# Block rows of a mixture of experts: loaded whole and turned by TensorE, or loaded in four shares and turned by VectorE

## The chip, the cores and the metric

The kernel runs on one core of one Trainium2 chip. The metric is the device time of one execution in microseconds, the lower the better. A core has five engines with an instruction queue each: PE (TensorE, matrix products; its weight loads are listed as PEld), DVE (VectorE), ACT (ScalarE), POOL (GpSimd) and SP (SyncE, which here issues DMAs). Each works its own queue in order and waits on semaphores that the others raise.

## The reference, cut to what matters

Everything is fp32. A layer on 8 x 512 tokens of width 256 runs through four residual parts: a linear scan, a mixture of experts, a causal attention with 16 heads, and the same mixture of experts again.

```python
x = x + _L0_attn_a_ref(_layernorm(x), ...)     # scan
x = x + _L0_ffn_ref(_layernorm(x), ...)        # mixture of experts, first time
x = x + _L0_attn_b_ref(_layernorm(x), ...)     # attention
x = x + _L0_ffn_ref(_layernorm(x), ...)        # mixture of experts, second time
```

A mixture of experts chooses 4 of 16 experts for every token, with a factor for each choice:

```python
h = jnp.einsum('td,edf->etf', x, gate_w)
u = jnp.einsum('td,edf->etf', x, up_w)
y = jnp.einsum('etf,efd->etd', jax.nn.silu(h) * u, down_w)
routed = jnp.einsum('etd,te->td', y, combine)      # combine: the factors, zero where not chosen
sh = jax.nn.silu(x @ sh_gate_w) * (x @ sh_up_w) @ sh_down_w
return routed + sh
```

Widths: 256 in, 256 inside an expert, 256 out.

## The kernel before, in words

Two stretches alternate with two routed stages. A stretch (the scan, later the attention) also norms the tokens, computes the shared expert and the choices, and sends each normed token row by an indirect DMA of POOL into the DRAM tensor `xg`, once for each of its four experts, so that the rows of one expert lie together. A row has `ROW` = 272 columns: 256 of the token, 4 factors, 4 expert numbers, 8 copies of the token's number.

A routed stage, `routed(i, ...)`, then goes through `xg` in blocks of `BLK` = 128 rows, each block of one expert. It runs 136 blocks (`LIKELY`; 7 more stand under a condition on the number of blocks that are needed). Where a block's rows lie and which expert's weights it takes is read from two small tables into registers (`values`, L830). For a block n:

- `load(n)` (L850): SP copies the 128 rows of 1,088 bytes from `xg` into a buffer `rows` with one row per partition. The buffers are those of the tag `kb4`, nine of them (`KB`), so block n takes that of block n - 9, whose scatter has to have landed.
- `fetch(n)` (L863): ScalarE copies the gate weights of the block's expert, VectorE the up weights, from the place in `w_all` that a register names into a fixed buffer (tag `col`, six buffers, so three blocks).
- `turn(n)` (L878): the products need the token's columns on the partitions. TensorE transposes the two halves of 128 columns into PSUM, `pt`, and ScalarE copies them into columns `ROW` and on of the same buffer.
- `up(n)` (L885): eight products 128x128x128 into `ph`, gate half and up half; ScalarE takes the sigmoid of the gate half (L901), VectorE multiplies twice (L902, L903), which makes `act`; VectorE forms the row factor, `gain`, from the row's factors and expert numbers (L906, L914).
- `down(n)` (L917): two products of `act` with the down weights into `pyr`, four passes on TensorE; ScalarE scales by `gain` (L929); POOL adds the rows to the DRAM tensor `part` by an indirect DMA (L930).

`run` (L940) writes these in the order load(n + 2), fetch(n + 1), up(n), turn(n + 1), down(n - 2), and some other work at given blocks (`beside`: norms for the next stretch, sums of finished tokens). That is the order of the program's text; the compiler's scheduler settles each engine's own order from it, except where `tc.issue_after` or `tc.keep_in_program_order` pins an instruction.

The 16 experts' weights are loaded whole into `w_all` by SP long before a routed stage (`load_expert`, L216): for the gate and up weights the input row 128 k + p goes to partition p, so each piece is one row of 1,024 bytes.

Of the kernel before, what the change touches and what calls it, by code (L numbers as in the profile page):

```python
# [31 lines left out]
EG, TKG, TK = 4, 2, 4  # L32
# [3 lines left out]
BLK = P  # L36


NBLK = (TK * NTOK - E) // BLK + E
# [3 lines left out]
LIKELY = TK * NTOK // BLK + E // 2  # L43
NROW = E * REG + BLK
ROW = D + 2 * TK + 8
# [13 lines left out]
PACE = 2  # L59
SENT = 4  # L60
HELD = 6


SUMMED = {0: DONE[0], 1: 76, 2: 88, 3: 110, 4: 127}
# [12 lines left out]
def tile_hybrid_block(  # L77
# [22 lines left out]
    nc = tc.nc  # L100
# [23 lines left out]
    xg = [dram.tile([NROW, ROW], FP, name=f"xg_{i}") for i in range(2)]  # L124
# [41 lines left out]
    ident = const.tile([P, P], FP, name="ident")  # L166
# [49 lines left out]
    def load_expert(e: int):  # L216
        at = e * WEXP
        gu = w_all[:, at : at + 2 * KD * F].rearrange("p (s k f) -> p s k f", k=KD, s=2)
        nc.sync.dma_start(out=gu[:, 0], in_=gate_w[e].rearrange("(k p) f -> p k f", p=P))
        nc.sync.dma_start(out=gu[:, 1], in_=up_w[e].rearrange("(k p) f -> p k f", p=P))  # L220
        nc.sync.dma_start(
            out=w_all[:, at + 2 * KD * F : at + WEXP].rearrange("p (k d) -> p k d", k=KF),
            in_=down_w[e].rearrange("(k p) d -> p k d", p=P),
        )
# [5 lines left out]
        out=before,  # L230
        in_=before,
# [20 lines left out]
    def load_attention_weights():  # L252
# [16 lines left out]
        out=causal, in_=causal, compare_op=ALU.is_ge, fill=0.0, base=0, pattern=[[0, 2], [1, P]], channel_multiplier=-1  # L269
# [6 lines left out]
        out=tri, in_=tri, compare_op=ALU.is_gt, fill=0.0, base=0, pattern=[[1, P]], channel_multiplier=-1  # L276
# [546 lines left out]
    def routed(i: int, table, beside):  # L823

        weight_at, row_at, expert, many, _ = table
        ACT, DVE = mybir.EngineType.Activation, mybir.EngineType.DVE
        PE, SP = mybir.EngineType.PE, mybir.EngineType.SP
        held = {}

        def values(n: int):  # L830

            many = min(4, (LIKELY if n < LIKELY else NBLK) - n)
            _, w = nc.values_load_multi_w_load_instructions(
                weight_at[:, n : n + many],
                engines=[PE, ACT, DVE],
                min_val=0,
                max_val=(E - 1) * WEXP,
                skip_runtime_bounds_check_because="a count of at most E - 1 experts, times WEXP",
            )
            _, r = nc.values_load_multi_w_load_instructions(  # L840
                row_at[:, n : n + many],
                engines=[SP],
                min_val=0,
                max_val=NROW - BLK,
                skip_runtime_bounds_check_because="the blocks table stays within the sorted rows",
            )
            for j in range(many):
                held[n + j] = [w[j], r[j]]

        def load(n: int):  # L850
            if n not in held:
                values(n)
# [7 lines left out]
            nc.sync.dma_start(out=rows[:, 0:ROW], in_=xg[i][bass.ds(held[n][1], BLK), :])  # L860
            held[n].append(rows)

        def fetch(n: int):  # L863


            if n == 0:

                both = xpool.tile([P, NT, D], FP, tag="x", name=f"both_{i}").rearrange("p t d -> p (t d)")
            for half, (copy, name) in enumerate(((nc.scalar.copy, "gate"), (nc.vector.tensor_copy, "up"))):
                if n == 0:  # L870
                    here = both[:, half * KD * F : (half + 1) * KD * F]
                    copy = nc.vector.tensor_copy
                else:
                    here = work.tile([P, KD * F], FP, tag="col", name=f"{name}_{i}_{n}", bufs=COLS)
                copy(here, w_all[:, bass.ds(held[n][0] + half * KD * F, KD * F)])  # L875
                held[n].append(here)

        def turn(n: int):  # L878
            rows = held[n][2]
            pt = bank([P, KD, P], f"pt_{i}_{n}", "misc")  # L880
            for k in range(KD):
                nc.tensor.transpose(pt[:, k, :], rows[:, k * P : (k + 1) * P], ident)  # L882
            nc.scalar.copy(rows[:, ROW : ROW + D], pt.rearrange("p k q -> p (k q)"))  # L883

        def up(n: int):  # L885
            _, _, rows, *both = held[n]


            ph = bank([P, 2, KF * P], f"ph_{i}_{n}", "big")
            for s in range(2):  # L890
                for f in range(KF):
                    for k in range(KD):
                        nc.tensor.matmul(  # L893
                            ph[:, s, f * P : (f + 1) * P],
                            lhsT=both[s][:, k * F + f * P : k * F + (f + 1) * P],
                            rhs=rows[:, ROW + k * P : ROW + (k + 1) * P],
                            start=(k == 0),
                            stop=(k == KD - 1),
                        )
            act = rows[:, ROW + D : ROW + D + F]  # L900
            nc.scalar.activation(act, ph[:, 0, :], AF.Sigmoid)  # L901
            nc.vector.tensor_mul(act, ph[:, 0, :], act)  # L902
            nc.vector.tensor_mul(act, ph[:, 1, :], act)  # L903

            gain = small.tile([P, TK + 1], FP, tag="gain", name=f"gain_{i}_{n}", bufs=4)
            nc.vector.scalar_tensor_tensor(  # L906
                gain[:, 0:TK],
                rows[:, D + TK : D + 2 * TK],
                expert[:, n : n + 1],
                rows[:, D : D + TK],  # L910
                ALU.is_equal,
                ALU.mult,
            )
            nc.vector.tensor_reduce(gain[:, TK : TK + 1], gain[:, 0:TK], AX.X, ALU.add)  # L914
            held[n][3:] = [act, gain]

        def down(n: int):  # L917
            w, _, rows, act, gain = held.pop(n)
            py = bank([P, D], f"pyr_{i}_{n}", "y")
            for f in range(KF):  # L920
                nc.tensor.matmul(  # L921
                    py,
                    lhsT=act[:, f * P : (f + 1) * P],
                    rhs=w_all[:, bass.ds(w + 2 * KD * F + f * D, D)],
                    start=(f == 0),
                    stop=(f == KF - 1),
                )

            nc.scalar.mul(rows[:, 0:D], py, gain[:, TK : TK + 1])  # L929
            nc.gpsimd.indirect_dma_start(  # L930
                out=parts[i][n % 2],
                out_offset=bass.IndirectOffsetOnAxis(
                    ap=rows[:, D + 2 * TK : D + 2 * TK + 1].bitcast(U32), axis=0
                ),
                in_=rows[:, 0:D],
                in_offset=None,
                compute_op=ALU.add,
            )

        def run(first: int, last: int):  # L940
            load(first)
            load(first + 1)
            fetch(first)
            turn(first)
            for n in range(first, last + 2):
                if n + 2 < last:
                    load(n + 2)
                if n + 1 < last:
                    fetch(n + 1)
                if n < last:  # L950
                    up(n)
                if n + 1 < last:
                    turn(n + 1)
# [12 lines left out]

    def shared_experts(i: int, b: int, xnT_of, tanh: bool):
# [454 lines left out]
    with banks_of(big=4, misc=2, y=2):  # L1422
# [68 lines left out]
        def at_the_end(b: int):  # L1491
# [4 lines left out]
            engines=[mybir.EngineType.SP, mybir.EngineType.Activation, mybir.EngineType.DVE],  # L1496
# [52 lines left out]
```

## Time and profile before

| | us |
|---|---|
| three runs | 1734.45, 1742.05, 1742.82 |
| median | 1742.05 |
| the profiled execution | 1735.83 |
| its span, first to last instruction | 1734.1 |

| part of the span | us from the start |
|---|---|
| scan stretch | 0 to 351 |
| routed stage 0, up products of 136 blocks | 351 to 741 |
| attention stretch | 741 to 1306 |
| routed stage 1 | 1306 to 1701 |
| last sums and stores | 1701 to 1734 |

The profile is one execution recorded by the hardware. A row of it names the line of the kernel, the engine, the operation, the tiles written and read, and the mean time of one instruction; the idle time in front of it is given with the engine or DMA that ended it. One fp32 matrix product appears as two passes. A busy share is a mean over stages with different limits, so the routed stages are read by themselves.

### The profile page before, as it was taken

How to read it: one execution, taken by the hardware profiler on the slowest of the kernel's cores; microseconds unless marked ns; L12 is line 12 of the kernel's file. 1: busy time of each engine (PE TensorE's matmuls, PEld its weight loads, DVE VectorE, ACT ScalarE, POOL GpSimd, SP SyncE). 2: the span in 40 equal slices, each digit the busy share in tenths (PEclk: the TensorE clock that was granted, in tenths of full speed). 3: DMA queues.
4: the chain of work that ended last, by engine and by line, in shares of the span. 5: the costliest groups of instructions: out<-in, count | busy, mean ns of one | idle time of the engine just before them, and what ended most of it. 6: DMA issues, size and time to landing. Idle time of an engine off the chain costs nothing. (4 is left out here: it accounts for less than half of the span.)

```text
span 1734.1 us, 32869 instructions
## 1 busy us (share of the span) xinstructions
PE 1648.4 (95%) x10640; PEld 1225.8 (71%) x10640; DVE 1110.7 (64%) x3463; ACT 788.7 (45%) x1724; POOL 773.0 (45%) x675
## 2 busy tenths in 40 slices
PE   6899998999999999999999999999998999998993
PEld 3566655589999999944445545544558999998992
DVE  7888877545556655566776676676754755565562
ACT  3223232155555555555544454364315555554551
POOL 3356556435555555530042332332543555555563
PEclk8999999999999999999999999999999999999997
DMA  4454423445555665531011212122544555566666
GB/s 160 147 179 151 148 93 121 153 95 95 96 95 104 105 101 95 106 62 38 25 65 50 77 51 72 55 73 84 192 138 89 96 96 97 111 138 124 122 120 166
DMA packets 149277, 181.37 MB, mean 105 GB/s; under 512 B 16144, under 2 KB 135984, under 8 KB 149104
## 3 DMA queue, kind: packets, MB, share of 16 engines
q0 software_dynamic: 54720, 82.57, 25.6%
q1 hardware_dynamic: 92576, 92.71, 17.9%
q10 hardware_dynamic: 1808, 3.93, 0.6%
q8 instruction: 89, 1.46, 0.4%
q14 instruction: 84, 0.69, 0.1%
HBM read 81.62 MB, written 97.53 MB: 103 GB/s over the span
## 5 line engine op out<-in xcount | busy, mean ns | idle before, releaser
L930 POOL DMA_INDIRECT part<-rows x272 | 425.9, 1566 | 341.5 <-ACT rows L929 236.7
L723 POOL DMA_INDIRECT xg<-sorted_m,slots_m x256 | 258.3, 1009 | 267.6 <-ACT slots_m L720 91.9
L893 PEld LDWEIGHTS ph<-rows,gate 128*128 128x128 f32 x2160 | 282.0, 191 | 16.1 <-ACT rows L883 1.9
L893 PE MATMUL ph<-rows,gate 128*128 128x128 f32 x2160 | 285.5, 275 | 0.6 <-ACT rows L883 0.6
L893 PE MATMUL ph<-rows,up 128*128 128x128 f32 x2160 | 285.3, 275 | 0.0
L921 PE MATMUL pyr<-w_all,rows 128*128 x1088 | 279.8, 380 | 0.4 <-DVE rstd_l L431 0.4
L893 PEld LDWEIGHTS ph<-rows,up 128*128 128x128 f32 x2160 | 262.9, 192 | 0.0
L901 ACT ACTIVATE rows<-ph 128x256 f32<-128x256 f32 x272 | 104.2, 383 | 328.5 <-PE ph L893 328.5
L902 DVE TENSOR_TENSOR rows<-ph,rows 128x256 f32<-128x256 f32 x272 | 115.2, 424 | 190.4 <-ACT rows L901 189.4
L921 PEld LDWEIGHTS pyr<-w_all,rows 128*128 128x128 f32 x1088 | 185.5, 190 | 14.9 <-ACT rows L929 0.8
L875 ACT COPY gate<-w_all 128x512 f32 x270 | 168.8, 626 | 14.2 <-PE ph L893 2.4
L1131 ACT ACTIVATE w_all<-ps_a 128x1024 f32<-128x1024 f32 x128 | 124.4, 1021 | 68.8 <-PE ps_a L1120 63.7
L875 DVE COPY up<-w_all 128x512 f32 x270 | 118.1, 437 | 30.3 <-PE ph L893 17.5
L929 ACT ACTIVATE rows<-pyr,gain 128x256 f32<-128x256 f32 x272 | 128.4, 472 | 14.3 <-PE pyr L921 12.2
L906 DVE SCALAR_TENSOR_TENSOR gain<-rows,expert_b 128x4 f32<-128x4 f32 x272 | 61.2, 225 | 107.9 <-ACT rows L929 82.4
L1120 PE MATMUL ps_a<-w_all 32*128 32x384 f32 (+3 forms) x1024 | 120.0, 468 | 8.0 <-ACT w_all L1131 6.3
L982 PE MATMUL pg_m<-xT_m,su_sb 128*128 128x512 f32 x256 | 123.4, 604 | 0.0
L982 PE MATMUL pg_m<-xT_m,sg_sb 128*128 128x512 f32 x256 | 122.3, 599 | 0.0
L903 DVE TENSOR_TENSOR rows<-ph,rows 128x256 f32<-128x256 f32 x272 | 115.0, 423 | 8.4
L1011 PE MATMUL pd_m<-sd_sb,act_m 128*128 128x256 f32 x512 | 120.0, 382 | 0.0
L1011 PEld LDWEIGHTS pd_m<-sd_sb,act_m 128*128 128x128 f32 x512 | 95.4, 190 | 22.0 <-issue 5.7
L882 PE MATMUL pt<-ident,rows 128*128 128x128 f32 x544 | 103.7, 273 | 6.2 <-DMA rows<-xg 4.8
(228 smaller groups left out, 2176.7 us busy)
## 6 DMA issues: line engine op xcount, KB each, us to landing
rows<-xg SPq DMA_DIRECT2D x272, 136.0 KB, 2.5
part<-x SPq DMA_DIRECT2D x16, 512.0 KB, 2.9
part<-ys_m SPq DMA_DIRECT2D x14, 512.0 KB, 3.1
w_all<-in_L_ffn_gate_w_dram SPq DMA_DIRECT2D x24, 256.0 KB, 5.4
w_all<-in_L_ffn_up_w_dram SPq DMA_DIRECT2D x24, 256.0 KB, 5.4
w_all<-in_L_ffn_down_w_dram SPq DMA_DIRECT2D x24, 256.0 KB, 5.8
sum<-part POOLq DMA_DIRECT2D x10, 512.0 KB, 4.1
xg<-zeros SPq DMA_DIRECT2D x34, 136.0 KB, 1.8
```

Source lines behind the costliest of these rows:

```text
L723: nc.gpsimd.indirect_dma_start(out=xg[i], out_offset=bass.IndirectOffsetOnAxis(ap=slots[:, at : at + 1], axis=0), in_=rows[:, t, :], in_of ...
L875: copy(here, w_all[:, bass.ds(held[n][0] + half * KD * F, KD * F)])
L893: nc.tensor.matmul(ph[:, s, f * P : (f + 1) * P], lhsT=both[s][:, k * F + f * P : k * F + (f + 1) * P], rhs=rows[:, ROW + k * P : ROW + (k ...
L902: nc.vector.tensor_mul(act, ph[:, 0, :], act)
L903: nc.vector.tensor_mul(act, ph[:, 1, :], act)
L921: nc.tensor.matmul(py, lhsT=act[:, f * P : (f + 1) * P], rhs=w_all[:, bass.ds(w + 2 * KD * F + f * D, D)], start=(f == 0), stop=(f == KF - 1),
L929: nc.scalar.mul(rows[:, 0:D], py, gain[:, TK : TK + 1])
L930: nc.gpsimd.indirect_dma_start(out=parts[i][n % 2], out_offset=bass.IndirectOffsetOnAxis(ap=rows[:, D + 2 * TK : D + 2 * TK + 1].bitcast(U ...
L982: made = nc.tensor.matmul(dst, lhsT=w[:, k, f * P : (f + 1) * P], rhs=xnT[:, k, :], start=(k == 0), stop=(k == KD - 1),)
L1011: nc.tensor.matmul(py[:, j, :], lhsT=acts[n][:, f, t * P : (t + 1) * P], rhs=shared[n][3][:, f, :], start=(n == 0 and f == 0), stop=(n == ...
L1120: nc.tensor.matmul(ps[j // 2][:, j % 2, col : col + n], lhsT=k_sb[w][r, o, c * P : (c + 1) * P], rhs=q_sb[r, o, c * P : T], start=True, st ...
L1131: nc.scalar.activation(es[two], ps[two][:, :, 0:cols], AF.Exp, scale=ATT_SCALE)
```

## The change

Rows are loaded so that VectorE can turn them. VectorE's transpose works on squares of 32x32. For every block but the first two of a `run` (`heads`), `load` issues four DMAs on SP, one per share of 64 columns: share a goes to the 32 partitions from 32 a on, and there the four groups of 32 rows lie side by side, so each piece is 256 bytes long. A fifth, small DMA on ScalarE's queue brings the last 16 columns, which hold the factors and numbers, in their old place, one row per partition. One VectorE transpose of 128x256 then makes what the two TensorE transposes and ScalarE's copy made; partition p holds columns 2 p and 2 p + 1 instead of p and 128 + p. The gate and up weights are loaded in the same arrangement, input rows 2 p and 2 p + 1 to partition p, in pieces of 2,048 bytes. The head blocks keep the whole load, TensorE's transposes (with every second column) and ScalarE's copy.

In `run`, rows are now loaded four blocks ahead (`AHEAD`) instead of two, and the turn is written two blocks ahead instead of one. The tables of row places are read for eight blocks at a time, for SP and ScalarE, apart from those of the weights, which are still read four at a time. The first instruction of `gain` is made to issue behind L903's second multiplication of the same block.

```diff
@@ load_expert
-        nc.sync.dma_start(out=gu[:, 0], in_=gate_w[e].rearrange("(k p) f -> p k f", p=P))
-        nc.sync.dma_start(out=gu[:, 1], in_=up_w[e].rearrange("(k p) f -> p k f", p=P))
+        nc.sync.dma_start(out=gu[:, 0], in_=gate_w[e].rearrange("(p k) f -> p k f", p=P))
+        nc.sync.dma_start(out=gu[:, 1], in_=up_w[e].rearrange("(p k) f -> p k f", p=P))
@@ routed
-        held = {}
+        held, heads, known = {}, set(), set()
...
+            for j in range(many):
+                held[n + j].insert(0, w[j])
+                known.add(n + j)
+
+        def places(n: int):
+
+            many = min(8, (LIKELY if n < LIKELY else NBLK) - n)
             _, r = nc.values_load_multi_w_load_instructions(
                 row_at[:, n : n + many],
-                engines=[SP],
+                engines=[SP, ACT],
...
-            nc.sync.dma_start(out=rows[:, 0:ROW], in_=xg[i][bass.ds(held[n][1], BLK), :])
+            block = bass.ds(held[n][-1], BLK)
+            if n in heads:
+                nc.sync.dma_start(out=rows[:, 0:ROW], in_=xg[i][block, :])
+            else:
+
+                for a in range(QUAD):
+                    nc.sync.dma_start(
+                        out=rows[a * SQ : (a + 1) * SQ, 0:D].rearrange("s (b c) -> s b c", b=QUAD),
+                        in_=xg[i][block, a * KD * SQ : (a + 1) * KD * SQ].rearrange("(b s) c -> s b c", s=SQ),
+                    )
+                nc.scalar.dma_start(out=rows[:, D:ROW], in_=xg[i][block, D:ROW])
@@ turn
-            pt = bank([P, KD, P], f"pt_{i}_{n}", "misc")
-            for k in range(KD):
-                nc.tensor.transpose(pt[:, k, :], rows[:, k * P : (k + 1) * P], ident)
-            nc.scalar.copy(rows[:, ROW : ROW + D], pt.rearrange("p k q -> p (k q)"))
+            xT = rows[:, ROW : ROW + D]
+            if n in heads:
+                pt = bank([P, KD, P], f"pt_{i}_{n}", "misc")
+                for k in range(KD):
+                    nc.tensor.transpose(pt[:, k, :], rows[:, 0:D].rearrange("p (q k) -> p k q", k=KD)[:, k], ident)
+                nc.scalar.copy(xT, pt.rearrange("p k q -> p (k q)"))
+            else:
+
+                nc.vector.transpose(
+                    xT.rearrange("p (k b s) -> p k b s", k=KD, b=QUAD),
+                    rows[:, 0:D].rearrange("p (b i k) -> p k b i", b=QUAD, k=KD),
+                )
@@ up
-            nc.vector.tensor_mul(act, ph[:, 1, :], act)
+            made = nc.vector.tensor_mul(act, ph[:, 1, :], act)
...
+            with tc.issue_after(made.ins):
+                nc.vector.scalar_tensor_tensor(
@@ run
-            load(first)
-            load(first + 1)
+            heads.update((first, first + 1))
+            coming = iter(range(first, last))
+
+            def load_to(n: int):
+                for m in coming:
+                    load(m)
+                    if m >= n:
+                        break
+
+            load_to(first + AHEAD - 1)
+            values(first)
             fetch(first)
             turn(first)
             for n in range(first, last + 2):
-                if n + 2 < last:
-                    load(n + 2)
+                load_to(n + AHEAD)
+                if n + 2 < last and n + 2 not in known:
+                    values(n + 2)
...
-                if n + 1 < last:
+                if n == first:
                     turn(n + 1)
+                if n + 2 < last:
+                    turn(n + 2)
```

In the changed kernel the lines shift: the four loads are L874, the small load L878, the VectorE turn L906, the up products L919, the sigmoid L927, the two multiplications L928 and L929, `gain` L933 and L941, the down products L948, the scaling L956, the scatter L957.

More of the change, by code (lines that the diff above doesn't have):

```diff
@@ L61 @@
 HELD = 6
+AHEAD = 4
 SUMMED = {0: DONE[0], 1: 76, 2: 88, 3: 110, 4: 127}
@@ L847, in values @@
             for j in range(many):
-                held[n + j] = [w[j], r[j]]
+                held[n + j] = [r[j]]
         def load(n: int):
             if n not in held:
-                values(n)
+                places(n)
             if n < 2:
@@ L902, in up @@
             nc.vector.tensor_mul(act, ph[:, 0, :], act)
-            nc.vector.tensor_mul(act, ph[:, 1, :], act)
+            made = nc.vector.tensor_mul(act, ph[:, 1, :], act)
             gain = small.tile([P, TK + 1], FP, tag="gain", name=f"gain_{i}_{n}", bufs=4)
[L906 to L913, printed above, removed]
+            with tc.issue_after(made.ins):
+                nc.vector.scalar_tensor_tensor(
+                    gain[:, 0:TK],
+                    rows[:, D + TK : D + 2 * TK],
+                    expert[:, n : n + 1],
+                    rows[:, D : D + TK],
+                    ALU.is_equal,
+                    ALU.mult,
+                )
             nc.vector.tensor_reduce(gain[:, TK : TK + 1], gain[:, 0:TK], AX.X, ALU.add)
```

## The prediction

> **What bounds the kernel now.** I read the page's busy shares and slices first, then the two routed stages (slices 9 to 17 and 31 to 40) by windows, then one block in the timeline.
>
> ```profile
> PE 1648.4 (95%) x10640; PEld 1225.8 (71%) x10640; DVE 1110.7 (64%) x3463; ACT 788.7 (45%) x1724; POOL 773.0 (45%) x675
> ...
> PE   6899998999999999999999999999998999998993
> ```
>
> TensorE is full nearly everywhere. The windows hold the 136 blocks of each stage:
>
> ```profile
> 351.00:741.00 390.00, 389.48 (x2982) 374.72 (x2983) 223.91 (x705) 212.87 (x537) 206.67 (x135) 1.00 0.58 98
> 1306.00:1701.00 395.00, 389.93 (x2974) 374.11 (x2975) 228.98 (x704) 214.71 (x536) 211.24 (x143) 1.00 0.61 110
> ```
>
> The first pair is TensorE's: 0.5 us idle of 390, 5 of 395. VectorE (fifth figure) is busy 57%, ScalarE 55%, DMA 58 to 61%, clock 1.00. In the timeline of one block (start, length, engine, line) the start of each engine's next work matters more than its busy time:
>
> ```profile
> 473.52 0.25 PEld L882 LDWEIGHTS pt<-ident,rows 128*128 128x128 f32 x2
> 473.63 0.38 PE L882 MATMUL pt<-ident,rows 128*128 128x128 f32 x2
> 473.74 0.73 PEld L921 LDWEIGHTS pyr<-w_all,rows 128*128 128x128 f32 x4
> 473.83 0.38 ACT L901 ACTIVATE rows<-ph 128x256 f32<-128x256 f32 x1 [1.10 <-PE ph L893]
> ...
> 474.25 0.42 DVE L902 TENSOR_TENSOR rows<-ph,rows 128x256 f32<-128x256 f32 x1 [0.68 <-ACT rows L901]
> ...
> 474.53 1.05 PEld L893 LDWEIGHTS ph<-rows,gate 128*128 128x128 f32 x8
> 474.70 0.42 DVE L903 TENSOR_TENSOR rows<-ph,rows 128x256 f32<-128x256 f32 x1
> ...
> 475.42 0.22 DVE L906 SCALAR_TENSOR_TENSOR gain<-rows,expert_b 128x4 f32<-128x4 f32 x1 [0.29 <-ACT rows L929]
> ...
> 475.68 0.16 DVE L914 TENSOR_REDUCE gain<-gain 128x1 f32<-128x4 f32 x1
> 475.81 0.43 DVE L875 COPY up<-w_all 128x512 f32 x1
> 476.39 0.25 PEld L882 LDWEIGHTS pt<-ident,rows 128*128 128x128 f32 x2
> ```
>
> A block takes 476.39 - 473.52 = 2.87 us, TensorE throughout: the turn 0.22 (473.52 to 473.74), the down product 0.87 (the chain of waits gives pyr x4 0.87), the up products 1.78 (ph x16). The sigmoid (L901) starts 0.31 after the last up pass is fed (473.52 to 473.83). It feeds L902 and L903, which end at 475.12. Nothing on TensorE waits for these now: the down product that follows is two blocks old.
>
> **What the Trainium skill says.** "VectorE: DVE Perf Modes", The three transpose paths: VectorE turns 32x32 blocks only; hence the four shares. It gives 311 ns for a bf16 128x128. The trace has an fp32 one:
>
> ```profile
> L606 DVE STREAM_TRANSPOSE logit_m<-pl_m x16: 302/316/319, 54.6 to 1255.1; 128x128 f32<-128x128 f32 x16
> ```
>
> "Trainium Architecture — The Big Picture", Inside one NeuronCore: engines run in parallel and meet only through semaphores. The trace agrees: L902 waited 0.68 us for the sigmoid with later VectorE work queued behind it. "DMA: Bandwidth & Descriptors", Why small descriptors are slow: a 256-byte piece takes 11 bus cycles, 3 of them overhead. No piece of block rows is under 1,088 bytes in this trace, so that is not shown.
>
> **The change, part by part.**
>
> *TensorE.* In each stage 134 blocks lose two passes, 0.22 us each: 2 x 134 x 0.22 = 59 us if nothing takes their place. Their ScalarE copies (0.37 us) go; they were hidden. The first two blocks of a stage keep both.
>
> *VectorE.* One transpose 128x256 per block. Price: L606's 0.316 plus 128 columns at 1.03 ns (128x512 and 128x256 tensor-tensor rows: 687 and 424 ns) = 0.45 us, an estimate; ends 0.41 (L440's 128x256 from SBUF) and 0.63 (twice L606). Sum per block 0.44 + 2 x 0.42 + 0.22 + 0.16 + 0.45 = 2.1 us, within 2.65. By busy time it is free. But where it stands in VectorE's queue decides, and the code's "two blocks ahead" is not what the compiled order has. That order, between L902 (m1) and L903 (m2) of a block, T being the turn, g and r the factors, U the up copy:
>
> ```
> before 40: m1-20 m2-20 g20 r20 U23 T22 | m1-21 m2-21 g21 U24 r21 T23
> later:     m1-104 T105 m2-104 g104 r104 U107 | m1-105 T106 m2-105 ...
> every 8th: m1-103 m2-103 g103 r103 T104 U106
> ```
>
> Counted over blocks 1 to 134 of both stages: in 97 the next block's turn precedes m1 (early, mostly the first 40 of a stage), in 153 it stands between m1 and m2, in 18 it comes behind the factors. In the last two kinds the turn cannot start before the current block's up products have ended, and the next up products wait for it. From the last pass of ph(n), with the timeline's steps:
> - sigmoid starts +0.31, ends 0.69; m1 starts 0.73, ends 1.15; T starts 1.18, ends 1.63; signal 0.05: ph(n+1) at 1.68 us. TensorE has only the down product between, 0.87 us, so it stands 0.81. Block: 1.78 + 1.68 = 3.46, **+0.59** on 2.87.
> - behind the factors: 1.18 + m2 0.42 + g 0.22 + r 0.16 + T 0.45 + three gaps and the signal 0.15 = 2.58; block 4.36, **+1.49**. Where TensorE has up to two down products there (1.74), they lie inside this.
> - early: 2.65, **-0.22**.
>
> Sum: 97 x -0.22 = -21; 153 x 0.59 = +90; 18 x 1.49 = +27; together +96 us. With T at 0.41 or 0.63: +89 or +127.
>
> *Row loads.* Five DMAs for one. SP issues four; an issue now takes
>
> ```profile
> L860 SPq DMA_DIRECT2D rows<-xg x272: 332/333/1797, 340.2 to 1692.9; - x136
> ```
>
> 0.33 and 0.07 of register work: 4 x 0.40 = 1.6 us of SP per block, under 2.65, nothing else queued. ScalarE issues the factors' load, 0.40 us, about what its lost copy gives back; its rows buffer is that of block n-9, whose scatter is by then some three blocks old (median 3.9 us to land), so the sigmoids and copies queued behind it should not be held. Cover gone: if scatters took over two blocks longer, ScalarE would hold the sigmoid. The compiled semaphores tie a block's fourth share to the landing of ScalarE's small load: two landings of 2.5 us plus an issue, 5.4 us, where about two slow blocks, 6.9, are available. Nothing, unless landings pass 3.2 us.
>
> *DMA engines.* Per block 640 row packets replace 128. A window of 50 us now:
>
> ```profile
> q0 software_dynamic: 2486, 2.26, 35.8%
> q1 hardware_dynamic: 2589, 2.50, 19.8%
> ```
>
> 19.8% of 800 us over 2589 packets is 61 ns each; the scatters take 286 us over 18 blocks, 1.0 us per block and engine. At the skill's 11 cycles against 35 for 1 KB, a 256-byte packet would take some 19 ns, an estimate, so rows about 0.7 us; at an unchanged 61 ns, 640 x 61 / 16 = 2.44. With the scatters 1.7 to 3.43 us; I take the middle, 2.6, under 3.46 and hidden. It cannot gain; its high end costs.
>
> *The rest.* Expert weights in 2 KB pieces land earlier, hidden (they load in other stages). Factors behind m2: off the path except in the 18 blocks. Row-table loads of 8 instead of 4, with one more on ScalarE (0.31 us per 8 blocks): hidden. Stage starts: more issues ahead of the first product, 1 to 2 us each, +3. VectorE's waits on four loads ahead of each turn: queue entries of 17 to 50 ns that may not overlap m1: 0 to 0.15 us on 171 blocks, 0 to 26 us; I take 8. Of the second stage's present stalls some 4 us go under the slower pace. POOL's instructions keep number and size, so nothing is queued newly there.
>
> Sum: 96 + 3 + 8 - 4 = +103 at the face; where kinds change, a block after a stalled one finds its turn and down product ready and stalls less; I take 7 off for the borders: **+96**. The profiled execution took 1735.8 us (span 1734.1, 1.7 around it), 6 under the median of three (1742.05). 1735.8 + 96 = 1832; of the 6 I take 4 for the median: **1836 us**.
>
> **Rivals.**
> - *TensorE stays the bound* (faster): every turn is done before it is asked for, in VectorE's queue at its idle time before L902. For it: VectorE's 2.1 us of work fits; against: 171 of 268 turns stand behind m1. Price -59 + 3 = 1680 (1686 for the median). It decides where fewer than 27% of turns are late (0.22 against 0.59 + 0.22), or where the hand-over takes under 1.09 us instead of 1.68; two of its four steps are measured at 0.42 and 0.38. Chance 8%.
> - *DMA is the bound*: at 61 ns a packet, 3.43 us in every block, early ones too, with stalls on top: 268 x 0.56 = +150, 1886. Half of that effect with the queue stalls is 1860. For it: five times the packets; against: the skill's cycles. 12%.
> - *The turn does not lead*, my forecast: 78%. That gains and stalls cancel: 2%.
>
> **How the numbers follow.** Faster 0.08, same 0.02, slower 0.90; half a per cent, 9 us, is about what a measurement can tell from no change. Range 1790 to 1880: below, T at 0.41 with every stall overlapping and no queue entries; above, T at 0.63 or dense DMA.
>
> **What would show it.** L906's transposes (134 per stage) at 0.41 to 0.63 us. Right: TensorE busy for nearly all of the first 40 blocks at 2.65 us each, then idle 0.8 us per block before L919 with the VectorE turn as releaser; ScalarE's sigmoid to turn to L919 recurring in the chain of waits. Wrong: up products every 2.65 us to the end, or turns waiting for DMA with the DMA share over 0.9.

## The result and the profile after

The kernel after takes 1833.08 us (median of 4 runs, 1829.62 to 1835.06) against 1739.61 for the kernel before on the same chip: a ratio of 1.0538, 95% interval 1.0514 to 1.0561. The forecast was 1836 and slower. The profiled execution took 1835.06 us with a span of 1833.3, so 99.2 us of span came on top of 1734.1.

The page of the kernel after, busy shares and TensorE's slices:

```profile
PE 1639.9 (89%) x10104; PEld 1156.5 (63%) x10104; DVE 1169.6 (64%) x3731; ACT 725.9 (40%) x1456; POOL 773.9 (42%) x675
...
PE   6899998899988888889999999999989998888884
```

The 8s of slices 12 to 18 and 34 to 39 lie in the two routed stages, whose first slices, 9 to 11 and 31 to 33, are still 9s. The windows of the two stages (length, then busy time of PE, PEld, DVE, ACT and POOL; at the end clock, DMA share, GB/s):

```profile
358.00:798.90 440.90, 385.08 (x2721) 341.41 (x2722) 250.75 (x833) 183.30 (x405) 211.74 (x138) 0.99 0.62 88
1368.70:1807.60 438.90, 383.70 (x2713) 340.45 (x2714) 256.16 (x839) 183.81 (x405) 220.18 (x148) 0.99 0.64 100
```

TensorE stands still for 56 and 55 us of them, where it stood for 0.5 and 5, and no engine is full: VectorE is busy 57 and 58%, DMA 62 and 64%. So it is a chain of waits across engines, not a bound of one of them. VectorE's timeline over two blocks shows the two late kinds (m1 is now L928, m2 L929, the turn L906):

```profile
682.92 0.42 DVE L928 TENSOR_TENSOR rows<-ph,rows 128x256 f32<-128x256 f32 x1 [0.80 <-ACT rows L927]
683.26 0.43 DVE L906 STREAM_TRANSPOSE rows<-rows 128x256 f32<-128x256 f32 x1
683.62 0.39 DVE L929 TENSOR_TENSOR rows<-ph,rows 128x256 f32<-128x256 f32 x1
...
686.32 0.42 DVE L928 TENSOR_TENSOR rows<-ph,rows 128x256 f32<-128x256 f32 x1 [0.88 <-ACT rows L927]
686.78 0.42 DVE L929 TENSOR_TENSOR rows<-ph,rows 128x256 f32<-128x256 f32 x1
...
687.57 0.45 DVE L906 STREAM_TRANSPOSE rows<-rows 128x256 f32<-128x256 f32 x1
```

and TensorE's timeline of the same time:

```profile
682.30 1.03 PE L948 MATMUL pyr<-w_all,rows 128*128 x4
683.84 1.13 PE L919 MATMUL ph<-rows,gate 128*128 128x128 f32 x8 [0.51 <-DVE rows L906]
...
688.29 0.38 PE L919 MATMUL ph<-rows,gate 128*128 128x128 f32 x2
```

In the first block the turn of the next block's rows sits between m1 and m2. It starts as m1 ends and releases the up products 0.58 us later (683.26 to 683.84). In the second it comes behind the factors, and the up products begin at 688.29, 4.45 us after the last ones. The costliest groups and the list of waits (total, times, longest) add this up:

```profile
L919 PE MATMUL ph<-rows,gate 128*128 128x128 f32 x2160 | 299.1, 281 | 99.0 <-DVE rows L906 84.6
...
L906 DVE STREAM_TRANSPOSE rows<-rows 128x256 f32<-128x256 f32 x268 | 117.0, 436 | 20.7 <-DMA rows<-xg 17.2
```

```profile
PE ph L919 <- DVE rows L906: 84.6, 130, 2.0
```

The turn itself hardly waits for its rows: 17.2 us in the whole run. So it is its place in the queue that makes it late, as the first experiment tests.

Taken apart at the first and the last load of up-product weights of each stage, with the main experiments beside it (us of the profiled span):

| kernel | up to the first | stage 1 | between | stage 2 | after the last | span |
|---|---|---|---|---|---|---|
| before | 351.2 | 390.0 | 564.7 | 395.3 | 32.8 | 1734.1 |
| after | 358.0 | 440.9 | 569.8 | 438.9 | 25.8 | 1833.3 |
| turn_early | 358.0 | 388.2 | 570.4 | 397.4 | 27.1 | 1741.0 |
| small_sp_alone | 350.8 | 512.8 | 567.2 | 509.2 | 24.8 | 1964.7 |
| small_sp_early | 351.6 | 414.1 | 564.4 | 418.6 | 24.5 | 1773.0 |
| whole_vector_near | 353.3 | 364.9 | 576.9 | 379.8 | 34.3 | 1709.2 |
| two_thirds_vector | 350.9 | 377.0 | 576.4 | 389.7 | 31.4 | 1725.3 |

94.5 of the 99.2 us are in the two stages.

### The profile page after: what moved, and what is told of

Its sections match the earlier page's. It is cut to its first block, busy times and chain, and to the rows that moved or that the text cites. A ratio compares the mean times of both kernels' runs of the same rounds, so it can differ in the third digit from the quotient of the medians.

```text
span 1833.3 us, 35597 instructions
## 1 busy us (share of the span) xinstructions
PE 1639.9 (89%) x10104; PEld 1156.5 (63%) x10104; DVE 1169.6 (64%) x3731; ACT 725.9 (40%) x1456; POOL 773.9 (42%) x675
## 5 line engine op out<-in xcount | busy, mean ns | idle before, releaser
L957 POOL DMA_INDIRECT part<-rows x272 | 427.6, 1572 | 434.9 <-DMA rows<-xg 203.3
L919 PE MATMUL ph<-rows,gate 128*128 128x128 f32 x2160 | 299.1, 281 | 99.0 <-DVE rows L906 84.6
L919 PEld LDWEIGHTS ph<-rows,gate 128*128 128x128 f32 x2160 | 270.1, 192 | 164.2 <-PE pyr L948 100.8
L948 PE MATMUL pyr<-w_all,rows 128*128 x1088 | 281.7, 381 | 13.1 <-DVE gain L933 13.1
L919 PE MATMUL ph<-rows,up 128*128 128x128 f32 x2160 | 285.3, 275 | 0.0
L927 ACT ACTIVATE rows<-ph 128x256 f32<-128x256 f32 x272 | 104.5, 384 | 430.6 <-PE ph L919 378.7
L919 PEld LDWEIGHTS ph<-rows,up 128*128 128x128 f32 x2160 | 262.9, 192 | 0.0
L928 DVE TENSOR_TENSOR rows<-ph,rows 128x256 f32<-128x256 f32 x272 | 114.7, 422 | 200.3 <-ACT rows L927 197.1
L948 PEld LDWEIGHTS pyr<-w_all,rows 128*128 128x128 f32 x1088 | 185.7, 191 | 35.3 <-ACT rows L956 19.1
L893 ACT COPY gate<-w_all 128x512 f32 x270 | 164.8, 613 | 37.3 <-PE ph L919 13.8
L956 ACT ACTIVATE rows<-pyr,gain 128x256 f32<-128x256 f32 x272 | 128.2, 473 | 54.1 <-PE pyr L948 19.6
L906 DVE STREAM_TRANSPOSE rows<-rows 128x256 f32<-128x256 f32 x268 | 117.0, 436 | 20.7 <-DMA rows<-xg 17.2
L929 DVE TENSOR_TENSOR rows<-ph,rows 128x256 f32<-128x256 f32 x272 | 109.0, 401 | 2.7
L1173 DVE SCALAR_TENSOR_TENSOR w_all<-w_all,causal 128x512 f32<-128x512 f32 (+1 forms) x128 | 70.8, 553 | 39.0 <-ACT w_all L1170 38.6
```

The costliest lines, as they stand in the source:

```text
L906: nc.vector.transpose(xT.rearrange("p (k b s) -> p k b s", k=KD, b=QUAD), rows[:, 0:D].rearrange("p (b i k) -> p k b i", b=QUAD, k=KD),)
L919: nc.tensor.matmul(ph[:, s, f * P : (f + 1) * P], lhsT=both[s][:, k * F + f * P : k * F + (f + 1) * P], rhs=rows[:, ROW + k * P : ROW + (k ...
L948: nc.tensor.matmul(py, lhsT=act[:, f * P : (f + 1) * P], rhs=w_all[:, bass.ds(w + 2 * KD * F + f * D, D)], start=(f == 0), stop=(f == KF - 1),
L957: nc.gpsimd.indirect_dma_start(out=parts[i][n % 2], out_offset=bass.IndirectOffsetOnAxis(ap=rows[:, D + 2 * TK : D + 2 * TK + 1].bitcast(U ...
```

## The experiments

Each ratio is to the kernel before on the run's own chip; the brackets hold the 95% interval.

**Is it the turn's place in VectorE's queue?** turn_early changes nothing but this place:

```diff
-                nc.vector.transpose(
+                turns[n] = nc.vector.transpose(
...
-            nc.vector.tensor_mul(act, ph[:, 0, :], act)
+            with tc.issue_after(turns[n + 1].ins) if n + 1 in turns else nullcontext():
+                nc.vector.tensor_mul(act, ph[:, 0, :], act)
```

> The changed kernel with one order added: the first multiplication of block n may issue only behind the VectorE turn of block n + 1, so that all 268 turns stand ahead of it in VectorE's queue. The same DMAs, the same instructions. Queue theory (the place of the turn in VectorE's queue costs the time): both stages go at TensorE's 2.65 us a block, some 360 us instead of 440.9 and 438.9, so 1833 - 155 = about 1680 us, below the kernel before. DMA rival (the 256-byte pieces cost it): nothing is taken from the DMA, so 1833 within 10. VectorE-work rival (0.44 us more per block on VectorE costs it): the same work, so 1833 within 10.

Measured: 1741.63 us, ratio to before 1.0015 (1.0002 to 1.0029). With the same transfers and the same work on every engine, 91 of the 93 us are gone: the place is the cause of the slowdown, and neither packets nor VectorE's load are, since both are unchanged. But the theory's further step, that TensorE would then run at 2.65 us per block, failed. The mean is 2.89 (median 2.70), so nothing is gained on the kernel before either. Its list of waits shows VectorE standing at the turn itself:

```profile
DVE rows L906 <- DMA rows<-xg: 66.7, 61, 5.3
```

**What if the turn costs twice as much?** turn_twice issues each transpose two times.

```diff
+                for _ in range(2):
                     nc.vector.transpose(
```

> The changed kernel with every VectorE turn made twice (the second rewrites the same values). The compiled order shifts with it: about 144 of the 268 pairs now stand wholly ahead of the first multiplication, about 106 have their first or second turn between or behind the multiplications in a way that holds the next up products, against 171 late turns in the changed kernel. Queue theory: some 23 us less in a stage, 1780 to 1800, faster although VectorE does 117 us more. VectorE-work rival: 268 x 0.44 = 117 us more, 1950. DMA rival: 1833 within 10.

Measured: 1855.99 us, 1.0670 (1.0633 to 1.0708). All three missed. 117 us of further VectorE work cost 23 us, so the time does not follow the work as such. Sorted by where the next block's two transposes stand in VectorE's queue, from one m1 to the next, 144 blocks with both ahead of m1 took 2.75 us, 48 with one ahead of m1 and one between the products 3.48, 58 with one between them and one behind m2 4.17, 18 with both behind the factors 4.80. The kinds stand in the order that the theory gives. Against the 2.87 us of before, the 124 late blocks cost 139 us and the early ones give back 17, where the stages grew by 118 in all. The expectation had counted on some 106 late blocks; what else made its range too low is not shown, as the block times behind it are not on record.

**The same lever pushed the other way.** small_sp_alone moves one cheap issue off ScalarE, and the scheduler answers with a worse order.

```diff
-                nc.scalar.dma_start(out=rows[:, D:ROW], in_=xg[i][block, D:ROW])
+                nc.sync.dma_start(out=rows[:, D:ROW], in_=xg[i][block, D:ROW])
```

> The kernel after with the block's 64-byte-piece load (row factors and places) issued by SP instead of ScalarE; same transfers, same instructions, no order forced. The compiled VectorE order changes by this much: of 134 turns per stage about 21-25 stand ahead of the first gating product (97 in the kernel after), 32-35 between the two products, 77-78 behind the row factors (18 in the kernel after). ORDER theory (the time is set by where the next block's turn stands in VectorE's queue; a block with an early turn 2.65 us, one between the products about 3.45, one behind the factors about 4.35 with the first of a run): replay of the three queues gives about 500 us per block stage against 434 for the kernel after, +130 in all: 1940 to 1970 us. LOAD rivals (DMA packets or VectorE's work set the loss; or ScalarE's in-order issue of the small load does): transfers and work are unchanged and ScalarE is relieved, so 1820 to 1835 or a little less.

Measured: 1966.60 us, 1.1319 (1.1292 to 1.1345), inside the order theory's 1940 to 1970. This is the sharpest test: the edit looks like a relief of ScalarE, and the forecast came from the compiled order alone. Both stages grew, to 512.8 and 509.2 us. The groups name the turn's place and what follows from it, the factors and m2 that a down product now waits for:

```profile
L948 PE MATMUL pyr<-w_all,rows 128*128 x1088 | 299.1, 390 | 164.4 <-DVE gain L933 83.4 <-DVE rows L929 76.2 <-ACT rows L956 3.1
L919 PE MATMUL ph<-rows,gate 128*128 128x128 f32 x2160 | 293.4, 279 | 78.9 <-DVE rows L906 52.4 <-ACT rows L956 17.2 <-DVE gain L933 5.0
```

The mean time of a block from its m1 to the next block's m1, sorted by where the next block's turn stands in VectorE's queue:

| next block's turn | predicted | after: blocks, us | small_sp_alone: blocks, us |
|---|---|---|---|
| ahead of m1 | 2.65 | 97, 2.72 | 46, 2.82 |
| between m1 and m2 | 3.46 | 153, 3.44 | 67, 3.45 |
| between m2 and the factors | none foreseen | 0 | 65, 3.94 |
| behind one or both factors | 4.36 | 18, 4.38 | 90, 4.36 |

The expectation counted the last two kinds as one. The prediction's own steps give 3.91 us for a turn right behind m2, an estimate made afterwards.

**Undoing the change's other half.** In whole_tensor_turn the loads are whole again and TensorE turns; the weights' order, the early loads and the factors' place stay. In whole_vector_turn the loads are whole and VectorE turns. It and the two later kernels with whole loads and VectorE's turn leave out the arrangement in shares, without which the 32x32 squares do not make a full turn: they tell times, and are no replacement.

```diff
-            if n in heads:                # in load, both kernels
+            if True:
...
-            if n in heads:                # in turn, whole_tensor_turn only
+            if True:
...
-                if n == first:            # in run, whole_tensor_turn only
+                if n + 1 < last:
                     turn(n + 1)
-                if n + 2 < last:
-                    turn(n + 2)
```

> The changed kernel with one part undone: every block, not only the first two, is loaded whole and turned by TensorE, one block ahead. What is left of the change: loads four blocks ahead, tables of eight, 2 KB weight pieces, the factors behind the second multiplication. Queue theory: TensorE at 2.87 us a block again, 1740 within 8. A rival in which one of these parts carries the loss (tables, look-ahead, factors): clearly above, 1760 to 1830.

> The changed kernel with whole loads for every block but VectorE's turn kept; the squares of a whole load are not arranged for it, so this leaves out the full turn of the rows and its numbers are not the reference's. In its compiled order all turns stand ahead of the first multiplication without being told. Queue theory: TensorE's 2.65 us a block, and no share loads at the start, 1665 to 1680. DMA rival: about the same, since the pieces are gone. VectorE-work rival: 268 x 0.44 us of work are still there, so 1740 or more. Together with the first run it says whether the share loads cost anything besides the order that they bring.

Measured: 1749.27 us, 1.0057 (1.0039 to 1.0075), and 1746.26 us, 1.0048 (1.0035 to 1.0061). The first is just above what was expected: loads four blocks ahead, 2 KB weight pieces and late factors together cost 10 us and are not the loss; in its profile the two stages are only 2 us longer than before, and 6.6 lie between them. The second misses by 66 us or more and lies where the rival of VectorE's work had put it. But the order there puts nearly all turns four or five blocks ahead, and VectorE, in order, stands at a turn whose rows have not landed. Their loads had waited in their turn, 557.8 us in 241 cases, for the scatters that free the buffers. VectorE's waits are these:

```profile
DVE rows L906 <- DMA rows<-xg: 256.8, 198, 5.1
```

So a turn can also be too early. If that is so, the same work in another place must take less; whole_vector_near holds it to one block ahead from both sides:

```diff
+                with tc.issue_after(mades[n - 2].ins) if n - 2 in mades else nullcontext():
+                    turns[n] = nc.vector.transpose(
...
+            with tc.issue_after(turns[n + 1].ins) if n + 1 in turns else nullcontext():
                 nc.vector.tensor_mul(act, ph[:, 0, :], act)
-            made = nc.vector.tensor_mul(act, ph[:, 1, :], act)
+            made = mades[n] = nc.vector.tensor_mul(act, ph[:, 1, :], act)
```

> whole_vector_turn (one whole load of 1,088-byte rows per block, turn by VectorE; the turn then orders a block's columns otherwise than the reference, so the output is not the reference's) with each turn forced to stand between the previous block's second product and the next block's first, instead of five blocks ahead as compiled there. LATE ROWS theory: at five blocks ahead VectorE waits at the turn for rows whose buffer a scatter has only just freed (256.8 us in 198 waits); one block ahead the rows are there, and with two transfers per block instead of six nothing else is late: 1675 to 1700. Rival SIDE WORK, or a bound of TensorE at about 2.87 us per block that the profile does not show: 1740 to 1746 as before.

Measured: 1709.72 us, 0.9838 (0.9817 to 0.9859): 37 us came with the turn's place alone, which speaks against VectorE's work as the price, though the time stayed 10 us above the upper end expected. Two windows of the first stage, one of the second:

```profile
400.00:500.00 100.00, 100.00 (x757) 96.09 (x756) 65.44 (x227) 51.51 (x115) 58.92 (x38) 1.00 0.63 104
...
600.00:700.00 100.00, 100.00 (x758) 96.16 (x757) 65.92 (x227) 50.64 (x114) 58.65 (x39) 1.00 0.63 104
...
1500.00:1600.00 100.00, 91.31 (x668) 85.75 (x667) 60.80 (x202) 45.44 (x102) 59.42 (x42) 0.98 0.67 130
```

TensorE is never idle in the undisturbed stretches, at 2.65 us per block: this is what the prediction's first rival describes, reached with whole loads and the turn in the right place. Of the 59 us that two lost passes are worth, 25 arrive in the first stage (390.0 to 364.9) and 15.5 in the second. There TensorE stands in part from 1500 on; its up products wait 8.7 us for VectorE in the window shown, and what held VectorE up was not followed further. 12.2 us are given back between the stages, where TensorE's work is the same. The windows of that stretch, of before and of whole_vector_near:

```profile
741.20:1305.90 564.70, 546.15 (x3459) 277.80 (x3457) 379.98 (x1211) 261.26 (x435) 164.85 (x164) 1.00 0.24 76
```

```profile
718.20:1295.10 576.90, 554.84 (x3459) 280.69 (x3457) 381.78 (x1215) 261.61 (x435) 166.01 (x165) 0.98 0.23 75
```

The same 3459 matmul records take 8.7 us longer at a granted clock of 0.98 instead of 1.00. The 0.98 is a mean: in the trace the clock is at half in three short stretches of that time, near 732, 745 and 1186 us, 24 us together, and nowhere in it in before.

**What limits turn_early?** Four runs look for the 31 us by which it lies above whole_vector_near. small_sp_early combines turn_early's and small_sp_alone's edits; small_sp_start adds to it that blocks 0 and 1 are loaded and block 0 is turned before further loads are issued.

> The run before it (small load on SP) with each next turn forced ahead of the first gating product, which was turn_early's edit. ORDER theory: the pin takes back all that the order cost, 1680 to 1745. What limits turn_early at 1741 instead of 1680: theory LATE ROWS (VectorE stands in order at a turn whose rows have not landed, 66.7 us in 61 places, because a share load waits for a completion slot that a small load holds which stands in ScalarE's queue): with the small load on SP the loads run ahead, the waits at the turn shrink, and the time falls to 1690-1720. Rival SIDE WORK (norms and sums of the shared part in VectorE's queue take what the turn takes): no change, 1735-1745. Rival SP ISSUE (five issues of 0.32 us, 1.6 us per block, become the bound or make rows later still): 1745-1770.

> small_sp_early with blocks 0 and 1 loaded and block 0 fetched and turned before the loads of blocks 2 and 3 are issued, as the kernel before does. START theory (the 6.8 and 5.0 us that each block stage begins later in the kernel after come from loads of later blocks standing ahead of the first block's copies): 8 to 12 us below small_sp_early. Rival: the start is set by the landing of the first rows or by the register values, not by those loads: 0 to 3 us below.

```diff
-            load_to(first + AHEAD - 1)
+            load_to(first + 1)
             values(first)
             fetch(first)
             turn(first)
+            load_to(first + AHEAD - 1)
```

Measured: 1778.52 us, 1.0249 (1.0229 to 1.0268), and 1776.53 us, 1.0247 (1.0226 to 1.0269). The first lies above every range expected, nearest to that of SP's issues. Rows ought to have come earlier without the small load in ScalarE's queue, and they come later: 143.8 us of waits at the turn instead of 66.7. SP's timeline in small_sp_early shows that the edit put a new limit in place of the one it was to test:

```profile
569.21 1.84 SPq L874 DMA_DIRECT2D rows<-xg  x4
571.24 0.35 SPq L878 DMA_DIRECT2D rows<-xg  x1
571.85 1.84 SPq L874 DMA_DIRECT2D rows<-xg  x4
```

A block's five issues take SP 2.64 us (569.21 to 571.85), a share every 0.51 with the register work between them. That is as long as TensorE's block and leaves SP no slack; a block takes 3.06 us on average. That each wait of SP is therefore lost for good fits this and is argued. The start theory falls too: both runs begin the first stage at 351.6. So it was the small loads on ScalarE that made the kernel after begin 6.8 us late: its first two stand in ScalarE's queue from 353.99 to 356.71, and the first block's weight copy behind them starts at 357.04. In small_sp_alone, whose only edit is to move these loads, it starts at 348.77.

four_whole_loads is whole_vector_near with four issues of 32 whole rows each, small_placed is turn_early with its small load held to an earlier place in ScalarE's queue, and besides with the turn pinned from both sides, small_sp_start's order of loads and a stage's first four small loads on SP.

```diff
-                nc.sync.dma_start(out=rows[:, 0:ROW], in_=xg[i][block, :])
+                for a in range(QUAD):     # four_whole_loads, from the third block on
+                    nc.sync.dma_start(
+                        out=rows[a * SQ : (a + 1) * SQ, 0:ROW], in_=xg[i][bass.ds(held[n][-1] + a * SQ, SQ), :]
+                    )
```

```diff
+            with tc.issue_after(muls[n - 6].ins):          # small_placed: a function of its own, behind down
+                smalls[n] = nc.scalar.dma_start(out=held[n][-1][:, D:ROW], in_=xg[i][block, D:ROW])
...
+            with tc.issue_after(smalls[n + 5].ins) if n + 5 in smalls else nullcontext():
+                muls[n] = nc.scalar.mul(rows[:, 0:D], py, gain[:, TK : TK + 1])
```

> whole_vector_near (turn by VectorE one block ahead, TensorE-bound at 1709.7 us) with each block's rows loaded in four shares of 32 whole rows, 1,088 bytes a piece, by SP, and no small load; the output is not the reference's, since the turn orders a block's columns otherwise. In this chip's traces one share takes SP 0.51 us (0.32 of issue and 0.19 of register work between), so four take 2.04 us per block instead of 0.57. ISSUE theory (turn_early's 31 us over whole_vector_near are the issues: rows land late because SP needs 2 us and more per block for them): 1725 to 1745 us. PIECES theory (they are the 256-byte and 64-byte pieces and the small load in ScalarE's queue): 1705 to 1715 us.

> turn_early (all blocks from the third on in four shares by SP and turned by VectorE) with the small load kept on ScalarE but held to one place in its queue, ahead of the eviction of the block five earlier (behind that of the block six earlier), where turn_early's compiled order has it one to three evictions later; the turn held between the previous block's second product and the next block's first; the first four small loads of a stage on SP and blocks 0 and 1 ahead of the others. The transfers of the steady blocks and their pieces are turn_early's. four_whole_loads has shown that four issues per block by SP cost nothing (1712). SMALL-LOAD theory (turn_early's 30 us over that are the small load: it stands in ScalarE's queue, and a share two blocks on waits for the completion slot it holds, so rows land behind their turn's place): the waits of the turn for rows fall from 66.7 us to under 25, and the time to 1708-1725, of which up to 8 by the start. PIECES theory (the 256-byte pieces land too late for nine row buffers): waits and time stay, 1730-1745.

Measured: 1712.11 us, 0.9863 (0.9832 to 0.9894), within the noise of whole_vector_near: four issues per block cost nothing that shows, and the issue theory falls. small_placed took 1777.51 us, on a chip on which the kernel before took 1768.31: 1.0065 (1.0044 to 1.0086), so it gains nothing on turn_early. The waits of the turn for its rows did fall, though not below 25,

```profile
L913 DVE STREAM_TRANSPOSE rows<-rows 128x256 f32<-128x256 f32 x268 | 117.5, 438 | 42.5 <-DMA rows<-xg 34.0 <-issue 6.9
```

but the stages took 389.8 and 398.4 us, as in turn_early, on a chip of which there is no profile of the kernel before. This does not clear the small load. TensorE now waited 22.1 us ahead of L956, the down product, for ScalarE's evictions, ahead of which that load now stands. And SP still stands at the shares until an earlier row load has landed, in turn_early (first line) as in small_placed (second), while the kernels with the small load on SP have at most 0.3 us of this wait:

```profile
SPq L874 <- DMA rows<-xg: 101.0, 84, 3.4
SPq L874 <- DMA rows<-xg: 74.5, 60, 3.4
```

What costs turn_early its 31 us is thus the 256-byte pieces, or the fifth transfer of every block with the waits that it brings to SP and ScalarE. These were not separated, and the cause **stays open**.

**A version that beats both.** half_vector and two_thirds_vector turn every second, or all but every third block on VectorE, the others whole on TensorE, with all loads on SP, small_sp_start's order of loads and whole_vector_near's two pins.

```diff
+        def whole(n: int):
+            return n in heads or n % 3 == 0        # n % 2 == 0 in half_vector
...
-            if n in heads:                         # in load and in turn
+            if whole(n):
```

> Even blocks loaded whole and turned by TensorE as before the change, odd ones loaded in shares and turned by VectorE, each such turn between the previous block's second product and the next block's first, all loads on SP. TensorE 2.65 + 0.11 us per block, SP 1.61 us per block on average (0.57 and 2.64). ORDER and ISSUE theories together: loads have slack again, 370.7 us per stage by the replay of the queues against 391 for the kernel before: 1695 to 1720. If share loads land late whatever SP's load: 1730 to 1745. If mixing costs new waits (ScalarE's copy, PSUM banks): over 1745.

> As half_vector, but only every third block whole: TensorE 2.65 + 0.07 us per block, SP 1.95 us per block on average, in runs of two share blocks of 2.64 us each. Replay 366.2 us per stage. ORDER and ISSUE theories: 1690 to 1720, below half_vector by up to 9 us if SP's 1.95 us still leaves the rows in time, above it if not. Late-whatever: 1735 to 1750.

Measured: 1736.29 us, 0.9988 (0.9973 to 1.0003), no difference from before; and **1731.32 us, 0.9961 (0.9948 to 0.9974)**, 0.4% faster than before and 5.5% than after. Both lie above what was expected of the theories, half_vector in the range named for shares that land late whatever SP's load. In its undisturbed stretches two_thirds_vector is TensorE's all the same, elsewhere not; two windows:

```profile
400.00:500.00 100.00, 100.00 (x762) 96.28 (x761) 62.23 (x210) 52.88 (x122) 56.55 (x37) 1.00 0.68 101
...
1500.00:1600.00 100.00, 93.11 (x671) 87.86 (x670) 58.59 (x185) 46.52 (x107) 58.16 (x42) 0.97 0.72 127
```

So share loads in two blocks of three, five transfers each, leave TensorE no wait in the first window. In the second its own turns wait 6.6 us for rows that are loaded whole (8.0 in half_vector, 4.8 in before). Nor do shares land late: between 400 and 700 in half_vector the DMA issues give size and median time to landing, and a share is not slower than a whole load:

```profile
rows<-xg SPq DMA_DIRECT2D x53, 136.0 KB, 2.8
rows<-xg SPq DMA_DIRECT2D x212, 32.0 KB, 2.4
```

The stages gained 13 and 6 us in two_thirds_vector, and 11.7 went between the stages, as above.

## Why the prediction was right

- **The order decides.** Right, and shown by turn_early and small_sp_alone. The trace has the three kinds in the same numbers, 97, 153 and 18. They measured 2.72, 3.44 and 4.38 us where 2.65, 3.46 and 4.36 stood. With the measured means, 97 x -0.15 + 153 x 0.57 + 18 x 1.51 = +100 us against +96; the stages grew by 94.5. Ahead of the up products TensorE stands 0.65 us a time (84.6 us in 130 waits) and not the 0.81 forecast, the down product before them being longer (1.03 us in the timeline, 0.87 taken). The chain of waits, named as a sign, says little: on the page it follows only a quarter of the span, and the turn has 1% of the span in it.
- **The turn's price.** 0.436 us measured, 0.45 taken. The hand-over in a block of the second kind, from m1 to the up products, is 0.92 us in the timeline (682.92 to 683.84), 0.95 in the prediction's steps (0.73 to 1.68).
- **DMA.** It went to the low end, not to the middle. In a window of 50 us of the kernel after:

```profile
q1 hardware_dynamic: 10660, 2.43, 27.7%
q10 hardware_dynamic: 2574, 0.15, 3.5%
```

27.7% of 800 us over 10660 packets is 20.8 ns for a packet of 256 bytes, 3.5% over 2574 is 10.9 ns for one of 64. The rows then take (512 x 20.8 + 128 x 10.9) / 16 = 0.75 us per block and engine, where the prediction's middle had 1.6 (2.6 less 1.0 for the scatters). The Trainium skill's cycle counts ("DMA: Bandwidth & Descriptors", Why small descriptors are slow), from which 19 ns was estimated for a 256-byte packet, agree with the 20.8 ns of the trace. The DMA rival's 61 ns does not occur.
- **SP's issues were mis-sized**: 0.51 us each, not 0.40, so 2.04 us per block, not 1.6. It did no harm at 3.4 us per block, as four_whole_loads shows even at 2.65; a fifth issue on SP leaves no slack at 2.65, as small_sp_early shows.
- **Stage starts were mis-sized**: +3 taken, +6.8 in the first stage. The step that was too small is "more issues ahead of the first product, 1 to 2 us each": ScalarE's first two small loads stand ahead of the first block's weight copy, which alone explains the delay, as small_sp_alone shows. Of the 5.1 us more between the stages, TensorE's busy time accounts for 3.1 (549.28 us against 546.15).
- **Not foreseen**: 7.0 us less after the last up product. Together, start +6.8, stages +94.5, between +5.1, end -7.0 make +99.4, the 99.2 but for rounding. That 1833 came so near to 1836 is in part luck: outside the stages +11.9 and -7.0 stand where +3 and nothing stood. Terms of the sum that no run separates: the queue entries (+8), the borders (-7) and the stalls (-4); the second stage grew 7 us less than the first.
- **The first rival** was rightly named and rightly turned down: it needs under 27% of late turns, and there were 64%. But its price of 1680 was too low even in whole_vector_near, where TensorE is full over long stretches (1709.7), as it assumed that every us saved on TensorE in a stage stays saved.

## What to carry to other kernels

When work moves from a busy engine to one with room, ask where it will stand in that engine's queue, and read it from the compiled order: "two blocks ahead" in the program text came out as between two dependent products, and moving one cheap issue cost 133 us through the order that came with it; one pin took 188 us off again (1966.60 to 1778.52). Pin a cross-engine producer from both sides, behind the consumer's last step and ahead of the next, because too late stalls the consumer and too early makes an in-order engine stand at data that has not landed. Then count the issues of the queue that feeds it against the new, shorter period.

## What was not expected of the hardware

- A 256-byte packet takes a third of the time of a 1,088-byte one (20.8 and 61 ns), a 64-byte packet a sixth (10.9): five times the packets raised the DMA engines' time per block from about 1.7 us (0.58 x 390 / 136) to 1.9 (0.68 x 388 / 136 in turn_early).
- A queue's issue costs more than its DMA instruction: 0.32 us, but 0.51 from one share to the next with the registers.
- The granted clock between the stages, where no kernel changed TensorE's work, was 1.00 in before, small_sp_early and small_sp_start and 0.98 to 0.99 in all others, in one profile each. whole_vector_near, four_whole_loads and the two mixed kernels gave back 10 to 12 us there. Each time it is short stretches at half, of 3 to 10 us, and not a clock that is a little lower throughout. What sets them off was not tried.
